# Layer norms spread into the stage before, a bound computed in pieces, buffers filled in pieces

## The chip, the cores and the metric

The kernel runs on one core of a Trainium2 chip. Its engines run in parallel, each with its own queue that is worked off in order: TensorE (PE: matmuls and transposes, with the load of its stationary operand shown apart as PEld), VectorE (DVE), ScalarE (ACT), GpSimd (POOL), and SyncE (SP), which here only starts DMA transfers. The metric is the device time of one execution in microseconds, the median of several.

## The reference, cut to what matters

Six layers are applied to x of 2 x 512 x 512 numbers in fp32, each behind a parameterless layer norm and with its input added back. In short:

```python
x = x + latent_attention_small(ln(x))   # 32 heads over latents of 12 and 4
x = x + ffn_lora(ln(x))                 # x @ W.T + bias, plus one adapter per batch
x = x + grouped_attention(ln(x))        # 32 heads of 128 in 8 groups, causal
x = x + ffn_lora(ln(x))
x = x + mla(ln(x))                      # 32 heads, low-rank q and kv, causal
x = x + ffn_moe(ln(x))                  # 8 adapters, the best 2 per row
x = x + attention_32x16(ln(x))          # 32 heads of 16, qkv bias, causal
x = x + ffn_moe(ln(x))
```

with

```python
def _layernorm(x, axis=-1, eps=1e-05):
    m = jnp.mean(x, axis=axis, keepdims=True)
    v = jnp.var(x, axis=axis, keepdims=True)
    return (x - m) / jnp.sqrt(v + eps)
```

The last attention masks with -66504 instead of minus infinity. Whether the masked entries can matter depends on the size of the weights: the kernel computes a bound from the norms of the q and k weights and takes one of two branches.

## The kernel before

x stays in on-chip memory as eight tiles of 128 rows by 512 (tiles 0 to 3 are the first batch, `b=0`; 4 to 7 the second). A **layer norm** of one tile (`layernorm`, L156 to L174) takes statistics on VectorE (L161, L163), an inverse square root (L179 on VectorE, L181 on POOL), xn = (x-m)*r on VectorE (L166, into one of two buffers), four 128x128 transposes on TensorE (L169), and a ScalarE copy into the shared room xT (L174). Every stage began with `layernorm_all`, all eight tiles in turn, and the LoRA, MoE and last-attention stages with `add_bias`, which adds the stage's output bias to x on POOL (L191). Chains of four accumulating matmuls go through `chain` (L150); their sum is added to x by VectorE in `add_to_x` (L194).

**Stages.** `attn_latent_small` works in 16 units (batch, half, i) under `run_quartets`, which interleaves scores of the next unit with exponents of this one; `divide`, `flatten` and `project` follow a unit as pieces. `ffn_lora` computes a coefficient from the start indices by seven small VectorE operations (L598 to L614), multiplies the adapter out (L619), adds it to the weight (L623) and runs one chain per tile. `attn_gqa` runs 16 (group, batch) steps m of four units j; `beside(m, j)` places values, outputs and keys between the units. `attn_mla` runs steps of eight heads h in the same manner. `ffn_moe` has a `front(t)` (router chain, the best two of eight on VectorE: L1051 to L1084) and a `back(t)` (transpose L1095, a chain of five), front one tile ahead of back. `causal_exact` (L1113) stands between MLA and the first MoE: it squares the two weights on POOL (L1131, 128x2048 each), sums over rows by two chains of four matmuls with a column of ones (`g_ones`), and leaves a flag. `attn_mha` first fills its rooms on POOL (qs, ks, vs, nm: L1179 to L1192), then per batch prepares q, k, v and runs `core`.

**What sets the order.** Inside `manual_schedule` blocks (the loops of the four attentions) TensorE's instructions stand in the order in which they are written; in MLA VectorE's also. Everything else is put in order by a planner that works with estimated durations and may move an instruction ahead of those written before it, but each engine still works its queue off in order. PSUM has eight banks, handed out by name (`proj`, `tr`, `sc`, `av`) or, inside the two big attentions, in turn (`hold`, `turn`, `release`). Large weights share five slots of 1 MB (tag w8), small ones six (w3); all loads are issued on SP's queue.

Of the kernel before, what the change touches and what calls it, by code (L numbers as in the profile page):

```python
# [38 lines left out]
P = 128  # L39
# [6 lines left out]
class Block:  # L46


    def __init__(self, ctx, tc, x, out):
# [10 lines left out]
        self.held = None  # L60

        self.x = []
        for t in range(NTILES):
            xt = self.const.tile([P, D], F32, tag=f"x{t}", name=f"x{t}")
            nc.sync.dma_start(out=xt, in_=x[t])
            self.x.append(xt)
# [10 lines left out]
        nc.gpsimd.memset(self.mhalf, -0.5)  # L77

# [77 lines left out]
    def layernorm(self, t, bank=None, back=False):  # L156

# [8 lines left out]
        nc.vector.tensor_scalar(xn, self.x[t], mv[:, 0:1], rstd, ALU.subtract, ALU.mult)  # L166
        tp = (bank or self.tr)()
# [7 lines left out]

    def inv_sqrt(self, v, scale, eps):

        ve = self.sm(1, "ve")
        self.nc.vector.tensor_scalar(ve, v, scale, eps, ALU.mult, ALU.add)  # L179
        r = self.sm(1, "rstd")  # L180
        self.nc.gpsimd.tensor_tensor(r, ve, self.mhalf, ALU.pow)  # L181
        return r

    def layernorm_all(self, bank=None, back=False):
        for t in range(NTILES):
            self.layernorm(t, bank, back)

    def add_bias(self, bias):

        for t in range(NTILES):  # L190
            self.nc.gpsimd.tensor_tensor(self.x[t], self.x[t], bias, ALU.add)  # L191
# [161 lines left out]
def attn_latent_small(k, a):  # L353
# [8 lines left out]
    with ExitStack() as ctx:  # L362
# [3 lines left out]
        wkvd = k.load(a["a_wkvd"], [P, KC, P], "w3", 6)  # L366
        wqk = k.load(a["a_wqk"], [P, 2, P], "a_wqk", 1, pool=lp)
# [84 lines left out]
        def fold_bias():  # L452
# [7 lines left out]
            k.add_bias(bias)  # L460

        folded = one([P, D], "folded")
        for piece in prepare(0):
            piece()
        extra = prepare(1) + [fold, fold_bias]
# [110 lines left out]

        with tc.manual_schedule(engines={mybir.EngineType.PE}):
            k.run_quartets(
                len(quartets), score, maxima, transposed, values, [divide, flatten, project], extra
            )  # L580


def ffn_lora(k, a):

# [3 lines left out]
    with ExitStack() as ctx:  # L588
# [6 lines left out]
        starts = k.load_row(a["f0_starts"], 4, "f0_starts", dtype=I32)  # L595
        rows = k.load(a["c_lora"], [P, 4], "c_lora", 1)

        startf = lp.tile([P, 4], F32, tag="startf", name="startf")  # L598
        nc.vector.tensor_copy(startf, starts)


        c = lp.tile([P, 4], F32, tag="le", name="le")
        nc.vector.tensor_scalar(c, startf, rows[:, 3:4], None, ALU.is_le)
# [938 lines left out]
```

## Time and profile before

| | |
|---|---|
| median of 3 runs | 2185.17 us (2184.05 to 2186.51) |
| profiled execution, its own time | 2187.9 us, span 2186.2 us, mean granted TensorE clock 0.98 |
| TensorE busy | 2083.8 us, 95% |
| VectorE, ScalarE, POOL busy | 1298.2, 731.3, 708.8 us |
| stages (start in us) | latent 0, LoRA 297, grouped 343, LoRA 1198, MLA 1244, bound and MoE 1738, last attention 1796, MoE 2125 |

A row of the view by stage has, behind the stretch, the busy time of each engine with the number of its instructions, then the granted clock as a share of full speed. A row of the timeline has start, duration, engine, line, operation, output and inputs, count, and in brackets how long the engine had been idle and what ended the idle time. A matmul in fp32 of 128 by 512 appears as two records. The whole in 40 slices, busy share in tenths:

```profile
PE   7999989999999999999998989999999889999988
PEld 3444444555555555555554444454544444554545
DVE  6678842655555555555555556666666584755745
ACT  2555621322222222222222155444544111541531
POOL 1100020423322222232322256555555436115211
```

### The profile page before, as it was taken

How to read it: one execution, taken by the hardware profiler on the slowest of the kernel's cores; microseconds unless marked ns; L12 is line 12 of the kernel's file. 1: busy time of each engine (PE TensorE's matmuls, PEld its weight loads, DVE VectorE, ACT ScalarE, POOL GpSimd, SP SyncE). 2: the span in 40 equal slices, each digit the busy share in tenths (PEclk: the TensorE clock that was granted, in tenths of full speed). 3: DMA queues.
4: the chain of work that ended last, by engine and by line, in shares of the span. 5: the costliest groups of instructions: out<-in, count | busy, mean ns of one | idle time of the engine just before them, and what ended most of it. 6: DMA issues, size and time to landing. Idle time of an engine off the chain costs nothing. (4 is left out here: it accounts for less than half of the span.)

```text
span 2186.2 us, 38883 instructions
## 1 busy us (share of the span) xinstructions
PE 2083.8 (95%) x15128; PEld 1094.9 (50%) x15128; DVE 1298.2 (59%) x3478; ACT 731.3 (33%) x2040; POOL 708.8 (32%) x945
## 2 busy tenths in 40 slices
PE   7999989999999999999998989999999889999988
PEld 3444444555555555555554444454544444554545
DVE  6678842655555555555555556666666584755745
ACT  2555621322222222222222155444544111541531
POOL 1100020423322222232322256555555436115211
PEclk9999989999999999999999999999999999999999
DMA  3000021112121212111010322010101102002001
GB/s 96 15 1 1 20 92 58 49 40 68 25 64 25 64 33 65 37 61 49 21 30 6 119 59 71 2 63 10 58 11 50 39 30 43 1 2 39 1 2 39
DMA packets 65751, 85.35 MB, mean 39 GB/s; under 512 B 13458, under 2 KB 50450, under 8 KB 60948
## 3 DMA queue, kind: packets, MB, share of 16 engines
q1 hardware_dynamic: 64916, 81.70, 12.6%
q8 instruction: 123, 2.02, 0.4%
q10 hardware_dynamic: 640, 1.05, 0.3%
q14 instruction: 72, 0.59, 0.1%
HBM read 58.60 MB, written 2.10 MB: 28 GB/s over the span
## 5 line engine op out<-in xcount | busy, mean ns | idle before, releaser
L239 ACT ACTIVATE room<-room,nmax 128x128 f32<-128x128 f32 (+3 forms) x384 | 211.2, 551 | 505.5 <-DVE nmax L229 504.5
L250 POOL TENSOR_SCALAR room<-room,invs 128x128 f32<-128x128 f32 (+3 forms) x384 | 198.0, 536 | 99.2 <-DVE invs L247 99.2
L677 POOL TENSOR_TENSOR q<-q,t 128x512 f32<-128x512 f32 x64 | 81.9, 1280 | 436.3 <-DVE t L676 436.3
L290 PE MATMUL sc<-turned,vals 32*128 32x128 f32 (+7 forms) x1058 | 190.6, 417 | 0.0
L290 PE MATMUL pj<-turned,vals 32*128 32x256 f32 (+7 forms) x692 | 189.0, 424 | 0.0
L290 PE MATMUL tp<-turned,vals 32*128 32x384 f32 (+7 forms) x676 | 158.8, 430 | 0.0
L218 PE MATMUL sc<-kT,q 128*32 128x256 f32 (+15 forms) x1576 | 145.6, 404 | 11.5 <-DVE invs L247 10.8
L263 DVE STREAM_TRANSPOSE turned<-room 128x1152 f32<-128x1152 f32 x80 | 107.9, 1363 | 73.1 <-POOL room L250 22.2
L290 PEld LDWEIGHTS sc<-turned,vals 32*128 32x128 f32 (+1 forms) x1058 | 126.3, 168 | 8.3 <-issue 5.6
L150 PE MATMUL pj<-room,w 128*128 128x512 f32 x272 | 122.2, 599 | 0.0
L181 POOL TENSOR_TENSOR rstd<-ve,mhalf 128x1 f32<-128x1 f32 x80 | 44.8, 562 | 205.3 <-DVE ve L179 192.4
L290 PEld LDWEIGHTS pj<-turned,vals 32*128 32x128 f32 (+1 forms) x692 | 107.1, 169 | 3.9 <-issue 2.2
L150 PE MATMUL sc<-w,room 128*128 128x512 f32 (+1 forms) x240 | 105.5, 582 | 0.0
L150 PE MATMUL sc<-room,w 128*128 128x512 f32 x232 | 105.2, 596 | 0.0
L290 PE MATMUL av<-turned,vals 32*128 32x256 f32 (+7 forms) x358 | 95.7, 420 | 8.8 <-DVE turned L263 8.8
L150 PE MATMUL sc<-w,ctxT 128*128 128x512 f32 x216 | 100.3, 607 | 2.2 <-ACT ctxT L304 2.2
L218 PE MATMUL tp<-kT,q 128*32 128x288 f32 (+15 forms) x1024 | 93.2, 398 | 2.9 <-POOL q L945 2.0
L290 PEld LDWEIGHTS tp<-turned,vals 32*128 32x128 f32 (+1 forms) x676 | 92.2, 169 | 4.4 <-issue 2.7
L239 ACT ACTIVATE probs<-probs,nmax 128x128 f32<-128x128 f32 (+3 forms) x128 | 71.1, 556 | 67.3 <-DVE nmax L229 66.0
L218 PEld LDWEIGHTS sc<-kT,q 128*32 128x32 f32 x1576 | 63.7, 110 | 58.4 <-issue 17.6
L218 PE MATMUL pj<-kT,q 128*32 128x256 f32 (+4 forms) x992 | 87.4, 386 | 4.9 <-DVE invs L247 4.1
L505 PE MATMUL sc<-qm,keys 32*128 32x512 f32 x200 | 86.8, 637 | 0.8 <-DVE qm L492 0.8
(564 smaller groups left out, 5768.8 us busy)
## 6 DMA issues: line engine op xcount, KB each, us to landing
vals<-v SPq DMA_DIRECT2D x256, 64.0 KB, 2.0
w<-in_b_wq SPq DMA_DIRECT2D x8, 1024.0 KB, 5.3
w<-in_b_wo SPq DMA_DIRECT2D x8, 1024.0 KB, 4.8
w<-in_m_wo SPq DMA_DIRECT2D x8, 1024.0 KB, 6.7
w<-in_f_w SPq DMA_DIRECT2D x4, 1024.0 KB, 4.8
w<-in_m_wqn SPq DMA_DIRECT2D x8, 384.0 KB, 3.1
x<-in_x SPq DMA_DIRECT2D x8, 256.0 KB, 4.6
w<-in_b_wk SPq DMA_DIRECT2D x8, 256.0 KB, 2.8
```

Source lines behind the costliest of these rows:

```text
L150: last = self.nc.tensor.matmul(out, lhsT, rhs, start=(i == 0), stop=(i == len(pairs) - 1))
L181: self.nc.gpsimd.tensor_tensor(r, ve, self.mhalf, ALU.pow)
L218: nc.tensor.matmul(ps[32 * i : 32 * i + 32, a - lo : b - lo], q[:, at : at + 32], keys[:, a:b], start=True, stop=True,)
L239: nc.scalar.activation(row, row, AF.Exp, bias=nmax, scale=-1.0, accum_out=total[:, qt : qt + 1])
L250: self.nc.gpsimd.tensor_scalar(row, row, inv[:, qt : qt + 1], 1.0, ALU.mult, ALU.mult)
L263: self.nc.vector.transpose(out[:, :last], probs[:, :last])
L290: self.nc.tensor.matmul(out[:, :, :n], values(i, j), rhs, start=(j == blocks[0]), stop=(j == stop[i]),)
L505: nc.tensor.matmul(ps, keys[b][rows[g], bass.ts(kc, P)], qm[u][rows[g]], start=True, stop=True)
L677: nc.gpsimd.tensor_tensor(out, out, t2, ALU.add)
```

## The change

The norm is split into `centred` (statistics and xn, optionally followed by the tile's bias add) and `place` (transposes and copy), and `layernorm_all` is gone. Tiles 0 to 3 of the next stage's norm are written into the end of the stage before: in the latent attention at units 7 to 9 of 16 (as the first batch is then complete), in the LoRA beside the chains of the second batch, in the grouped attention and MLA at the last step, in the MoE beside the second batch's tiles, in the last attention before the second `core`. Tiles 4 to 7 follow inside the stage itself. Bias adds go tile by tile. Only four tiles of x are loaded first; the other four behind two weights. The masks are built after the first `prepare`.

The LoRA coefficient is kept for the second use. PSUM banks are held in turn from the first LoRA to the end of MLA.

The bound becomes a class: its weights are loaded in the middle of the grouped attention, squared and summed over the four blocks on POOL in place, a piece per step, and one matmul with ones for each weight does the sum over rows. The flag is read before the last attention. The last attention's rooms are taken before the first MoE, which fills an eighth of each per tile on POOL.

```diff
-        self.x = []
-        for t in range(NTILES):
-            xt = self.const.tile([P, D], F32, tag=f"x{t}", name=f"x{t}")
-            nc.sync.dma_start(out=xt, in_=x[t])
-            self.x.append(xt)
+        self.coef = None
+        self.x = [
+            self.const.tile([P, D], F32, tag=f"x{t}", name=f"x{t}") for t in range(NTILES)
+        ]
+        self.source = x
+        self.load_x(0)
...
+        self.ones = self.const.tile([P, 1], F32, tag="ones", name="ones")
+        nc.gpsimd.memset(self.ones, 1.0)
+    def load_x(self, b):
+        for t in range(b * NT, b * NT + NT):
+            self.nc.sync.dma_start(out=self.x[t], in_=self.source[t])
+    def masks(self):
+        nc = self.nc
...
-    def layernorm(self, t, bank=None, back=False):
+    def centred(self, t, bias=None):
...
+        if bias is not None:
+            self.add_bias(t, bias)
+        return xn
+    def place(self, t, xn, bank=None, back=False):
+        nc = self.nc
...
+    def layernorm(self, t, bank=None, back=False, bias=None):
+        self.place(t, self.centred(t, bias), bank, back)
...
-    def layernorm_all(self, bank=None, back=False):
...
-    def add_bias(self, bias):
-        for t in range(NTILES):
-            self.nc.gpsimd.tensor_tensor(self.x[t], self.x[t], bias, ALU.add)
+    def add_bias(self, t, bias):
+        self.nc.gpsimd.tensor_tensor(self.x[t], self.x[t], bias, ALU.add)
...
+        k.load_x(1)
...
         for piece in prepare(0):
             piece()
+        k.masks()
...
+        normal = {}
+        def norms(u):
+            i = u - len(quartets) // 2 + 1
+            if i in (1, 2):
+                for t in (2 * i - 2, 2 * i - 1):
+                    k.place(t, normal.pop(t), k.turn)
+            if i in (0, 1):
+                for t in (2 * i, 2 * i + 1):
+                    normal[t] = k.centred(t)
+        after = [divide, flatten, project, norms]
         with tc.manual_schedule(engines={mybir.EngineType.PE}):
-            k.run_quartets(
-                len(quartets), score, maxima, transposed, values, [divide, flatten, project], extra
-            )
+            k.run_quartets(len(quartets), score, maxima, transposed, values, after, extra)
...
-        starts = k.load_row(a["f0_starts"], 4, "f0_starts", dtype=I32)
-        rows = k.load(a["c_lora"], [P, 4], "c_lora", 1)
-        startf = lp.tile([P, 4], F32, tag="startf", name="startf")
-        nc.vector.tensor_copy(startf, starts)
-        c = lp.tile([P, 4], F32, tag="le", name="le")
-        nc.vector.tensor_scalar(c, startf, rows[:, 3:4], None, ALU.is_le)
-        r = lp.tile([P, 3], F32, tag="rank", name="rank")
-        both = lp.tile([P, 2], F32, tag="both", name="both")
-        nc.vector.tensor_tensor(both, c[:, 1:3], c[:, 2:4], ALU.mult)
-        nc.vector.tensor_tensor(r[:, 0:2], c[:, 1:3], both, ALU.subtract)
-        nc.vector.tensor_copy(r[:, 2:3], both[:, 1:2])
-        nc.vector.tensor_tensor(r, r, rows[:, 0:3], ALU.mult)
-        coef = lp.tile([P, 1], F32, tag="coef", name="coef")
-        nc.vector.tensor_reduce(coef, r, AX.X, ALU.add)
-        nc.vector.tensor_scalar(la, la, coef, None, ALU.mult)
+        if k.coef is None:
...
+            nc.vector.tensor_reduce(k.coef, r, AX.X, ALU.add)
+        nc.vector.tensor_scalar(la, la, k.coef, None, ALU.mult)
...
-            out = [k.sc() for b in range(B)]
+            out = [k.turn() for b in range(B)]
...
-        k.layernorm_all()
-        k.add_bias(bias)
+        for t in range(NT):
+            k.add_bias(t, bias)
         for b in range(B):
             for t in range(NT):
-                ps = k.proj()
+                ps = k.turn()
                 k.chain(
                     ps, [(k.xT[b][:, c, bass.ts(t, P)], adapted[b][:, c]) for c in range(KC)]
                 )
                 k.add_to_x(b * NT + t, ps)
-def attn_gqa(k, a):
+                if b == 0:
+                    k.layernorm(NT + t, k.turn, bias=bias)
+                else:
+                    k.layernorm(t, k.turn, back=True)
...
-        k.hold()
-        k.layernorm_all(k.turn, back=True)
         ckvT = []
         for b in range(B):
+            if b:
+                for t in range(NT, NTILES):
+                    k.layernorm(t, k.turn, back=True)
...
+            if m == len(groups) and j in (1, 2):
+                for t in (2 * j - 2, 2 * j - 1):
+                    k.layernorm(t, k.turn)
...
+            for at, n in ((4, "q"), (9, "k")):
+                if (m, j) == (at, 2):
+                    bound.begin(n)
+                if m == at + 1:
+                    bound.square(j)
+                if (m, j) == (at + 2, 0):
+                    bound.sum()
+            if (m, j) == (12, 0):
+                bound.end()
...
-            k.hold()
-            k.layernorm_all(k.turn, back=True)
             for t in range(NTILES):
                 b, tt = divmod(t, NT)
+                if b == 0:
+                    k.layernorm(NT + t, k.turn, back=True)
...
+            last = m == len(groups)
+            if last and h == 0:
+                rows.extend(k.centred(t) for t in range(2))
+            if last and h == 1:
+                for t in range(2):
+                    k.place(t, rows[t], k.turn)
+                rows.extend(k.centred(t) for t in range(2, NT))
+            if last and h == 4:
+                for t in range(2, NT):
+                    k.place(t, rows[t], k.turn)
...
-        k.layernorm_all()
-        k.add_bias(bias)
+        for t in range(NT):
+            k.add_bias(t, bias)
...
-        prev = None
-        for t in range(NTILES):
-            hw = front(t)
-            if prev is not None:
-                back(*prev)
-            prev = (t, hw)
-        back(*prev)
...
-def ffn_moe(k, a, last=False):
+def ffn_moe(k, a, last=False, beside=lambda t: None):
...
+        rows = {}
+        for t in range(NTILES + 1):
+            if t < NTILES:
+                rows[t] = front(t)
+                beside(t)
+            if t < NT:
+                k.layernorm(NT + t, bias=bias)
+            if t > 0:
+                back(t - 1, rows.pop(t - 1))
+            if t > NT and not last:
+                k.layernorm(t - 1 - NT)
+class CausalBound:
...
+    def begin(self, n):
+        k = self.k
+        self.w = k.load(self.a["h_w" + n], [P, KC, D], "w8", 5)
+        self.row = k.w.tile([P, D], F32, tag="bias", name="bound", bufs=1)
+        k.nc.sync.dma_start(out=self.row[:1], in_=self.a["h_r" + n])
+    def square(self, c):
+        mul = lambda t: self.k.nc.gpsimd.tensor_tensor(t, t, t, ALU.mult)
+        mul(self.w[:, c])
+        if c:
+            self.k.nc.gpsimd.tensor_tensor(self.w[:, 0], self.w[:, 0], self.w[:, c], ALU.add)
+        else:
+            mul(self.row[:1])
+            self.k.nc.gpsimd.tensor_tensor(
+                self.w[:1, 0], self.w[:1, 0], self.row[:1], ALU.add
             )
+    def sum(self):
+        k = self.k
+        ps = k.turn()
+        k.chain(ps[:1], [(k.ones, self.w[:, 0])])
+        norm = k.sm(H, f"bound{len(self.norms)}", 1)[:1]
+        k.nc.vector.tensor_reduce(
+            norm, ps[:1].rearrange("p (h d) -> p h d", h=H), AX.X, ALU.add
+        )
+        self.norms.append(norm)
+    def end(self):
+        k, nc = self.k, self.k.nc
+        norm = self.norms[0]
+        nc.vector.tensor_tensor(norm, norm, self.norms[1], ALU.mult)
+        nc.vector.tensor_scalar(norm, norm, self.LIMIT, None, ALU.is_lt)
+        every = k.sm(1, "ve")[:1]
+        nc.vector.tensor_reduce(every, norm, AX.X, ALU.min)
+        self.flag = k.const.tile([1, 1], I32, tag="bound_flag", name="bound_flag")
+        nc.vector.tensor_copy(self.flag, every)
+    def register(self):
+        return self.k.nc.values_load(self.flag[0:1, 0:1], min_val=0, max_val=1)
+class HeadRooms:
...
+    def fill(self, i):
+        pool = self.k.nc.gpsimd
+        pool.memset(self.q[:, i], 0.0)
+        pool.tensor_copy(self.kk[:, i], self.column.broadcast_to([P, S]))
+        n = self.v.shape[1] // 8
+        pool.memset(self.v[:, i * n : (i + 1) * n], 1.0)
+        pool.memset(self.nm[i // 4][:, i % 4], 0.0)
...
+        for t in range(NT):
+            k.add_bias(t, bo)
...
             rotated(b, wq, bq, q, (nc.sync, nc.sync))
+            if b == 0:
+                for t in range(NT, NTILES):
+                    k.layernorm(t, bias=bo)
             last = rotated(b, wk, bk, kk, (nc.sync, nc.scalar))
...
             prepare(b)
+            if b:
+                for t in range(NT):
+                    k.layernorm(t)
...
     attn_latent_small(k, a)
+    bound = CausalBound(k, a)
+    k.hold()
     ffn_lora(k, a)
-    attn_gqa(k, a)
+    attn_gqa(k, a, bound)
     ffn_lora(k, a)
     attn_mla(k, a)
-    exact = causal_exact(k, a)
-    ffn_moe(k, a)
-    attn_mha(k, a, exact)
+    with k.tc.tile_pool(name="heads", bufs=1) as pool:
+        rooms = HeadRooms(k, a, pool)
+        ffn_moe(k, a, beside=rooms.fill)
+        attn_mha(k, a, bound.register(), rooms)
     ffn_moe(k, a, last=True)
```

## The prediction

> **What bounds the kernel.** I read the busy shares first (TensorE 2083.8 of 2186.2 us, 95%: at most 102.4 us of idle time can be won, plus what a lowered clock and removed work cost), then the busy time by stage, then the list of what TensorE waited for, then the timeline at each stage boundary. The stages, with columns start:end, length, then busy time of PE, PEld, DVE, ACT, POOL, the granted clock, DMA share and GB/s:
>
> ```profile
> 0.00:297.30 297.30, 276.62 (x1760) 123.80 (x1761) 207.80 (x366) 150.75 (x284) 24.93 (x39) 0.98 0.08 25
> ...
> 378.90:1198.30 819.40, 815.35 (x5924) 452.17 (x5921) 439.20 (x1030) 192.99 (x656) 240.58 (x345) 1.00 0.15 42
> 1198.30:1243.90 45.60, 42.13 (x113) 20.54 (x112) 27.09 (x56) 4.59 (x8) 12.42 (x14) 0.89 0.38 125
> ...
> 1738.50:1796.00 57.50, 52.75 (x196) 27.57 (x195) 45.84 (x176) 8.21 (x23) 14.82 (x16) 1.00 0.03 7
> 1796.00:1843.50 47.50, 40.20 (x109) 19.74 (x107) 24.09 (x35) 9.98 (x16) 42.25 (x28) 0.89 0.26 54
> ```
>
> The grouped attention (second row) has TensorE busy 99.5% of the time: nothing to win inside. The short stages are the ones with gaps and a clock below 1. The waits say who ends the gaps (total us, times, longest):
>
> ```profile
> PE tp L169 <- DVE xn L166: 17.2, 7, 6.7
> PE pj L169 <- DVE xn L166: 12.0, 3, 11.3
> ...
> PE av L290 <- DVE turned L263: 8.8, 2, 6.9
> ```
>
> 29.2 us stand ahead of the norm's transposes (L169): at a stage's head nothing but norms is ready. The 6.9 has another cause, on the timeline where the latent attention (MLA) ends (start, duration, what, idle before):
>
> ```profile
> 1704.58 3.60 POOL L1131 TENSOR_TENSOR room<-w 128x2048 f32<-128x2048 f32 x1 [2.23 <-DVE invs L247]
> ...
> 1708.16 2.06 POOL L250 TENSOR_SCALAR probs<-probs,invs 128x128 f32<-128x128 f32 x4
> ...
> 1711.68 1.11 PE L290 MATMUL av<-turned,vals 32*64 32x512 f32 x1 [6.89 <-DVE turned L263]
> ```
>
> A 3.60 us square for the bound (L1131) came ahead of the last softmax scaling on POOL's queue.
>
> **The change, boundary by boundary** (one norm: TensorE 0.44 us for four transposes; VectorE 0.69+0.18+0.14+0.54 = 1.55, with 0.55 on POOL between; a four-matmul chain of 512 columns 3.43).
>
> *Start.* TensorE first runs at 11.27 (the 11.3 above): VectorE takes statistics of several tiles (L161, up to 10.08) before its first xn at 10.68. Four tiles loaded first: about 3 us earlier, of which the deferred norms (4 x 1.55 on VectorE) give back 2 in the loop. **-1.**
>
> *Latent loop, norms of the next stage.* Added: 4 x 0.44 = 1.75 on TensorE and 4 x 1.55 = 6.2 on VectorE over three units. Between 131 and 300 us VectorE is busy 124 of 169 us and TensorE 162: a unit of about 14 us has 3.7 us of VectorE to spare, 11 over three, so the sum fits, but the transposes stand in a hand-written TensorE order and can wait. Ends: 1.75 (fits) and 10 (two groups each waiting some 4). By the row nearest (a maximum awaited for 1.9 us once), **+4.**
>
> *Into the first LoRA.* Idles 0.53 and 1.0 and 1.1 on L169 and cold clock (stage mean 0.85, about 4 us) for norms that will be done; the coefficient chain stays the first time. **-3.** *Into the grouped attention:* one idle of 0.75; **-0.5.**
>
> *Grouped attention into the second LoRA.* Between 1171 and 1216 about 14.9 us are lost: waits 1.87 and 2.17, half-clock stretches 1.7 and 1.8, 2.8 for norms behind the coefficient's small operations (L603, L606, L609), some 4.6 cold around L619 (8 matmuls 3.75, then 4.50). Kept coefficient and early norms remove the 2.8 and most of the last; the 1.87 stays; four norms fill most of the 2.17. I leave 8.2: **-6.7.** Here a rule is weighed. The clock rows:
>
> ```profile
> 1182.78 5.40 PE L150 MATMUL sc<-w,ctxT 128*128 128x512 f32 x8 [2.17 <-ACT ctxT L304]
> 1188.02 3.60 PE L150 MATMUL pj<-w,ctxT 128*128 128x512 f32 x8
> ```
>
> The Trainium skill ("TensorE: Matmul & The Clock Gate", Part 1) says that the clock halves after an idle window of about 3.4 us; by it a 2.17 us gap need cost nothing beyond itself, and this boundary would give -4.9. The row shows 1.8 us lost after a gap of 2.17; I follow the row.
>
> *The bound inside the grouped attention.* Two one-matmul sums replace two chains (7.03 us in 16 records at 1737.14): 7.03/4 = **+1.7** of TensorE there, and 18 POOL operations of 1.28 (the row of L677, same shape) = 23 us. Hidden: POOL is busy 241 of 819 us and the squares come one per step. A scaling delayed by 2 x 1.28 would show as a TensorE wait; taken as 0. Its two weights take one of the five w8 slots and shift their ring by one: the next group's wo then waits for the output of the group two back, which ends a step before, and lands 4.8 us later (row of in_b_wo), a step ahead of need, at a DMA share of 0.15: nothing. Likewise at nothing: the masks built later on POOL (their first reader is 300 us away), the second half of x behind two weights on SP's queue (0.25 MB a tile, 4.6 us, needed a unit later), the register read moved past the first MoE (its flag is then 500 us old).
>
> *Second LoRA into MLA.* Eight norms stand ahead of the first chain's end at 1251; afterwards the four of the second half lie between chains paced 3.4 us by the small operations. **-3.**
>
> *MLA, bound, first MoE, head of the last attention* (1703.7 to 1811). The square leaves POOL: 6.89 becomes about 3.3, **-3.6**, the scaling and turn themselves being late next. The bound's chains: **-7.0**, with their small VectorE work behind which norms waited (0.77 and 1.78, the latter on g_flag): **-2.** Norms of the last attention go into the MoE loop; at 1796 they cost:
>
> ```profile
> 1795.86 3.52 POOL L1179 MEMSET qs<- 128x4096 f32 x1 [1.91 <-PE sc L150]
> ...
> 1796.44 6.94 DVE L166 TENSOR_SCALAR xn<-x,ln_mv,rstd 128x512 f32<-128x512 f32 x2
> 1799.31 3.79 POOL L1181 COPY ks<-c_spare 128x4096 f32<-128x4096 f32 x1
> 1799.80 0.63 PE L169 MATMUL tp<-ident,xn 128*128 128x128 f32 x4 [3.13 <-DVE xn L166]
> ...
> 1803.53 1.09 PE L169 MATMUL tp<-ident,xn 128*128 128x128 f32 x4 [3.10 <-DVE xn L166]
> ```
>
> Idles 3.13+3.10+1.07, about 4 of cold clock, 1.75 of transposes: the gap to close is **-13**. But the MoE loop pays. Where it already carries a norm per tile it runs at 6.36 us a tile (hw transposes at 1764.42 and 1770.78), against 5.33 of TensorE (front 0.93, back 4.40). Before, some tiles carry none; after, all eight do: about **+6** with the first router chain of some 5 us now uncovered. The fills add 3.52+3.79+2.22+1.54 = 11.07 us of POOL, 1.38 a tile. The second rule is weighed here, the one that speaks against the change: the skill ("SBUF — State Buffer", Who interferes with whom) says that POOL and a two-port VectorE operation lock each other out for a whole instruction. By it every fill could be paid, 8 x 1.38 = 11. The rows agree on the mechanism (xn 3.47 each here, 0.51 elsewhere), but in the loop just one operation per tile shows it: hotp takes 1.00 beside a 1.27 bias add, 0.23 without. 8 x 0.5 = **+4.** Sum -15.5, ends -7 and -23.
>
> *Last attention and second MoE.* Four norms beside the second prepare: +1.75 of TensorE, where it is full (41.30 of 41.30). After the last attention TensorE stood 6.66 us for a norm (2132.51) and then ran cold; about 5 of it stays, for the first router chain is now what is late; norms of tiles 4 to 7 lie in the loop. **-3.**
>
> **Sum:** -1+4-3-0.5-6.7+1.7-3-15.5-3 = -27.0. From the profiled execution's 2187.9 (span 2186.2 and 1.7 around it): 2160.9; that run lies 2.7 above the median of the runs shown (2185.17), so the median goes to **2158**; the forecast's own range is 2147 to 2170. No change means within 0.2%, 4.4 us, which is about what a measurement of this kernel can tell.
>
> **Rivals.**
> 1. *Mostly given back* (chance 0.18): the latent loop costs 10, fills 10, the LoRA heads keep part of their cold clock (4 less won): -27+6+6+4 = -11, **2174**. For it: VectorE's 45.84 of 57.5 in MoE. Against: VectorE's spare time in the latent loop.
> 2. *Everything hidden* (0.15): fills free (-4), latent loop 1.75 (-2), both MoE at TensorE's 5.33 a tile (12 tiles with norms x 1.0, -12), boundary before the second LoRA clean (-5): -27-23 = -50, **2135**. Against: the 6.36 a tile that exists already.
> 3. *Slower* (0.08): norms put into the hand-written TensorE order stand in it until xn is there, and everything behind stands too. Seven such groups (two in the latent loop, two where grouped attention ends, two where MLA ends, one before the second core). At the 6.66 seen at 2132.51 each: 7 x 6.66 = 46.6, net +20, **2205**. It decides from (27+4.4)/7 = 4.5 us each. Against: statistics start as soon as x is complete, a step ahead of the transposes.
> 4. *It does not do what it says* (0.05): the order outside the hand-written parts is planned, and statistics are hoisted already (L161 at 1171.16, before the last values); two xn buffers then hold the norms where they were. Only the bound's 7 and the kept coefficient's 2 remain, less its sums' 1.7, 1.75 before the second core and 4 of fills: -1.5, **2184**, no change.
>
> **Chances.** Forecast 0.54. Faster: 0.54+0.18+0.15 = 0.87; same 0.05; slower 0.08. Range 2136 to 2177: it takes in most of rival 1 and the near half of rival 2, leaving out rivals 3 and 4 and the rest.
>
> **What would show it.** Right: first transposes near 8; none of the three L169 waits above 3 us left but the last MoE's; no chain with g_ones, and the last MLA wait about 3.3; MoE tiles near 6.4 to 6.9; the last attention's head at clock 1. Wrong: waits on xn inside the latent or grouped loops; MoE tiles above 8 us; softmax scaling late beside the bound's squares.

## The result, and the profile after

| | before | changed |
|---|---|---|
| median, beside each other | 2185.84 us (2184.05 to 2188.02, 4 runs) | 2155.49 us (2154.52 to 2156.56, 4 runs) |
| profiled execution: its own time, span | 2187.9, 2186.2 | 2156.43, 2154.7 |
| mean granted TensorE clock | 0.980 | 0.987 |
| TensorE busy | 2083.8 | 2068.3 |

The ratio is 0.9861, 95% interval 0.9844 to 0.9878: 30 us faster. The forecast was 2158. A second comparison of the same two kernels gave 0.9834 (0.9818 to 0.9851). A difference of some 0.003, 6 us, between medians therefore says little here; for the small steps I go by the trace, and compare times from one landmark to the next, not absolute ones. Where an edit leaves a short stretch alone, such a time comes back: from MLA's last query to the last attention's first score, the nine traces in which that stretch is unedited lie between 143.4 and 143.5 us. The long loops vary more, by up to 5 us.

Busy time by stage, changed kernel (columns as in the view shown of before; the stretches are grouped attention, second LoRA, first MoE, second MoE):

```profile
378.50:1197.70 819.20, 816.20 (x5943) 451.80 (x5940) 443.57 (x1041) 194.99 (x660) 264.13 (x366) 1.00 0.16 46
1197.70:1232.00 34.30, 34.30 (x109) 16.42 (x109) 20.56 (x45) 4.11 (x7) 5.73 (x8) 1.00 0.48 167
...
1720.60:1772.60 52.00, 46.32 (x181) 26.19 (x180) 42.35 (x167) 7.83 (x23) 25.09 (x47) 1.00 0.03 6
...
2092.90:2150.60 57.70, 49.52 (x161) 27.32 (x160) 33.91 (x151) 5.67 (x20) 7.17 (x8) 0.88 0.09 33
```

The second LoRA went from 45.60 us at clock 0.89 to 34.30 us at clock 1.00, with TensorE busy throughout. The last stage still runs at 0.88. TensorE's waits (total us, times, longest), changed kernel:

```profile
PE pj L186 <- DVE xn L175: 11.6, 1, 11.6
...
PE tp L186 <- DVE xn L175: 4.8, 2, 4.3
PE sc L650 <- DVE w L643: 4.7, 1, 4.7
```

Of 29.2 us of waits for xn, 16.7 are left (0.3 of it in a row not shown), nearly all at the very start (11.6) and at the head of the second MoE (4.3). The third row is new: the adapter's products of the first LoRA (L650) wait for VectorE's scaling of A (L643).

Where the 31.4 us between the two spans came from, from landmark to landmark of the two traces:

| stretch | before | changed | measured | forecast |
|---|---|---|---|---|
| start to the first latent score | 26.47 | 28.97 | +2.5 | -1 |
| latent attention | 270.84 | 273.03 | +2.2 | +4 |
| first LoRA | 45.80 | 41.26 | -4.5 | -3 |
| head of the grouped attention | 35.87 | 35.28 | -0.6 | -0.5 |
| grouped attention, bound's sums in it | 819.34 | 819.12 | -0.2 | +1.7 |
| second LoRA | 45.58 | 34.34 | -11.2 | -6.7 |
| head of MLA, to its third query | 46.76 | 47.88 | +1.1 | -3 |
| MLA to its last output | 446.24 | 440.67 | -5.6 | -3.6 |
| bound's chains and first MoE | 58.70 | 52.05 | -6.6 | -9 +6 +4 = +1 |
| head of the last attention, to its first score | 55.70 | 44.23 | -11.5 | -13 |
| last attention, second MoE | 334.8 | 337.9 | +3.1 | -3 |

The sum was off by some 4 us, but its terms by up to 7.6, in both directions: they err by 15 us on the one side and by 19 on the other, and that these nearly cancel is luck.

### The profile page after: what moved, and what is told of

It reads as the page before. It is cut to its first block, busy times and chain, and to the rows that moved or that the text cites. A ratio compares the mean times of both kernels' runs of the same rounds, so it can differ in the third digit from the quotient of the medians.

```text
span 2154.7 us, 38870 instructions
## 1 busy us (share of the span) xinstructions
PE 2068.3 (96%) x15116; PEld 1085.4 (50%) x15116; DVE 1281.2 (59%) x3467; ACT 728.8 (34%) x2040; POOL 719.2 (33%) x988
## 5 line engine op out<-in xcount | busy, mean ns | idle before, releaser
L305 PE MATMUL sc<-turned,vals 32*128 32x256 f32 (+7 forms) x1004 | 187.3, 420 | 0.0
L305 PE MATMUL tp<-turned,vals 32*128 32x384 f32 (+7 forms) x742 | 170.9, 411 | 0.0
L305 PE MATMUL pj<-turned,vals 32*128 32x384 f32 (+7 forms) x754 | 146.8, 416 | 3.1 <-DVE turned L278 3.1
L233 PE MATMUL sc<-kT,q 128*32 128x160 f32 (+15 forms) x1536 | 139.5, 399 | 8.6 <-DVE invs L262 7.9
L278 DVE STREAM_TRANSPOSE turned<-room 128x1152 f32<-128x1152 f32 x80 | 108.0, 1363 | 66.4 <-POOL room L265 22.1
L305 PEld LDWEIGHTS sc<-turned,vals 32*128 32x128 f32 (+1 forms) x1004 | 122.5, 167 | 6.2 <-issue 4.1
L305 PEld LDWEIGHTS tp<-turned,vals 32*128 32x128 f32 (+1 forms) x742 | 102.9, 167 | 5.0 <-issue 2.7
L305 PEld LDWEIGHTS pj<-turned,vals 32*128 32x128 f32 (+1 forms) x754 | 97.8, 169 | 11.8 <-DVE turned L278 5.8
L233 PE MATMUL tp<-kT,q 128*32 128x224 f32 (+15 forms) x1032 | 92.4, 392 | 6.9 <-DVE invs L262 6.9
L233 PE MATMUL pj<-kT,q 128*32 128x512 f32 (+4 forms) x992 | 92.7, 407 | 2.9 <-POOL q L993 1.9
L160 PE MATMUL sc<-w,ctxT 128*128 128x512 f32 x192 | 87.5, 598 | 0.0
L265 POOL TENSOR_SCALAR probs<-probs,invs 128x128 f32<-128x128 f32 (+3 forms) x128 | 65.6, 532 | 61.3 <-DVE invs L262 57.4
```

The lines of the kernel that those rows point to most:

```text
L160: last = self.nc.tensor.matmul(out, lhsT, rhs, start=(i == 0), stop=(i == len(pairs) - 1))
L233: nc.tensor.matmul(ps[32 * i : 32 * i + 32, a - lo : b - lo], q[:, at : at + 32], keys[:, a:b], start=True, stop=True,)
L265: self.nc.gpsimd.tensor_scalar(row, row, inv[:, qt : qt + 1], 1.0, ALU.mult, ALU.mult)
L278: self.nc.vector.transpose(out[:, :last], probs[:, :last])
L305: self.nc.tensor.matmul(out[:, :, :n], values(i, j), rhs, start=(j == blocks[0]), stop=(j == stop[i]),)
```

## The experiments

All edits are to the changed kernel. The ratio is to the kernel before, run beside each.

| run | edit | median us | ratio (95%) |
|---|---|---|---|
| c0 | none | 2153.29 | 0.9834 (0.9818 to 0.9851) |
| e1 | bound whole again, behind MLA | 2168.05 | 0.9901 (0.9885 to 0.9918) |
| e2 | fills whole again | 2161.74 | 0.9869 (0.9852 to 0.9885) |
| e3 | MLA's norms ahead of its chains | 2150.40 | 0.9824 (0.9807 to 0.9840) |
| e4 | three banks for the adapter | 2160.67 | 0.9866 (0.9850 to 0.9882) |
| e5 | last MoE's norms back at its head | 2153.95 | 0.9843 (0.9826 to 0.9859) |
| e6 | second LoRA's norms back at its head | 2155.24 | 0.9845 (0.9828 to 0.9861) |
| e7 | second batch's norms held at the start | 2153.81 | 0.9848 (0.9830 to 0.9867) |
| e8 | last attention's norms back at its head | 2158.51 | 0.9854 (0.9838 to 0.9871) |
| e9 | coefficient computed twice | 2159.32 | 0.9864 (0.9848 to 0.9881) |
| e11 | three edits together | 2147.20 | 0.9805 (0.9789 to 0.9822) |
| e12 | the three, placed better | 2143.30 | 0.9797 (0.9783 to 0.9811) |

**e1, the bound.** The pieces in the grouped attention are dropped, and `causal_exact` of before stands again ahead of the first MoE:

```diff
-                if m == at + 1:
-                    bound.square(j)
...
+    exact = causal_exact(k, a)
     ffn_moe(k, a, beside=rooms.fill)
```

> The changed kernel (2155.5), but the bound computed where it was, between MLA and the first MoE, in two chains of four with POOL squares of 128x2048. Theory: the move was worth 7.0 us of chains and about 3.6 us of the scaling that stood behind the square, less 1.7 us of sums in the grouped attention: 8.9 slower, about 2164; a MLA wait on the turned probabilities near 6.9 us comes back. Rival (the chains lay beside waits for norms that are gone, so little is lost): at most 4 slower, below 2160.

The first transposed router result (hw) of the MoE came 13.9 us after its place in the changed kernel, the span grew by 10.7, and this ratio's interval alone of the undoing runs lies above both of the changed kernel's. POOL's and TensorE's timeline where MLA ends, in e1:

```profile
1691.88 3.60 POOL L1243 TENSOR_TENSOR room<-w 128x2048 f32<-128x2048 f32 x1 [2.86 <-DVE invs L262]
1695.46 2.05 POOL L265 TENSOR_SCALAR probs<-probs,invs 128x128 f32<-128x128 f32 x4
...
1698.98 1.11 PE L305 MATMUL av<-turned,vals 32*64 32x512 f32 x1 [4.79 <-DVE turned L278]
```

and in the changed kernel:

```profile
1692.82 2.05 POOL L265 TENSOR_SCALAR probs<-probs,invs 128x128 f32<-128x128 f32 x4 [2.96 <-DVE invs L262]
...
1696.34 0.64 PE L305 MATMUL pj<-turned,vals 32*64 32x512 f32 x1 [1.28 <-DVE turned L278]
```

In e1 POOL was free at 1691.88 and took the square first; the last scaling stood behind it. TensorE's wait for that value (L305 on `turned`, L278) is 4.8 in e1 and 1.3 in the changed kernel. Behind the wait a record of the same shape takes 1.11 us instead of 0.64: the granted clock is 0.50 from there to 1703.9 in e1, and 1.00 throughout this place in the changed kernel. By stretches, e1 is 7.4 us longer from MLA's last query to its last output, 7.3 longer from there to the first hw, and 2.0 shorter from the first hw to the last. Of the 7.4, 3.5 are the longer wait, 1.4 a new wait for an xn, and some 2.4 the clock (an estimate: half of the 4.9 us at half clock). So 12.8 us are lost up to the last attention's first score. The theory holds in kind, and was too small: it had 8.9, with a wait near 6.9 and no loss of clock.

**e2, the fills.** `beside=rooms.fill` goes, and the rooms are filled whole at the head of the last attention, as before; only their allocation stays ahead of the MoE:

```diff
+        nc.gpsimd.memset(q, 0.0)
+        nc.gpsimd.tensor_copy(
+            kk.rearrange("p t s -> p (t s)"), rooms.column.broadcast_to([P, 8 * S])
+        )
...
-        ffn_moe(k, a, beside=rooms.fill)
+        ffn_moe(k, a)
```

> The changed kernel, but the rooms of the last attention filled whole at its head, not an eighth per MoE tile. Theory (my step: fills cost 4 in the MoE loop, and at the head 11 us of POOL stand ahead of the bias adds and the rotation): MoE shorter by about 4, head longer by 4 to 8, 0 to 4 slower, about 2157. Rival (each fill locks VectorE out for its whole length, 8 x 1.38): the MoE loop gets 11 shorter and the kernel about 5 faster, 2150.

The edit did not put the fills back where they had been: the planner moved them by itself to the MoE's beginning, since their rooms were free there. In e2's timeline (start, duration):

```profile
1730.82 3.60 POOL L1275 COPY ks<-c_spare 128x4096 f32<-128x4096 f32 x1
1730.87 3.56 DVE L1132 SCALAR_TENSOR_TENSOR rest<-hotp,p 128x8 f32<-128x8 f32 x1
```

and in the changed kernel's:

```profile
1729.00 0.79 POOL L1255 COPY ks<-c_spare 128x512 f32<-128x512 f32 x1
...
1729.25 0.56 DVE L1118 TENSOR_SCALAR hotp<-cand,first 128x8 f32<-128x8 f32 x1
```

A VectorE operation on eight columns, 0.15 to 0.23 us elsewhere, ends with POOL's copy in both: it waits as long as that copy lasts. Behind a piece the wait is at most 0.8. In e2 TensorE waited 5.66 us for the first router result, in the changed kernel 2.58. From MLA's last query to the first score e2 took 146.5 us against 143.4: compared with whole fills in the MoE, the pieces are worth some 3 us. What whole fills at the attention's head would cost beside early norms, as both theories had it, no run shows. Another 3.7 of e2's longer span (2163.3) came between MLA's first and last query, where its trace shows a granted clock of 0.76 against 0.95 over the first 34 us, and which the edit does not touch. Its median alone tells nothing.

**e8, norms of the last attention.** The norms written beside the first MoE's second batch go back to the next head, fills stay in pieces:

```diff
-            if t > NT and not last:
-                k.layernorm(t - 1 - NT)
...
-            k.add_bias(t, bo)
+            k.layernorm(t, bias=bo)
```

> The changed kernel, but the last attention's norms of tiles 0 to 3 written at its own head, not into the first MoE's second half; fills stay in pieces. Theory (what made the old head slow was the whole fills on POOL, xn 3.47 beside them and 0.51 otherwise, not where the norms stood): 0 to 3 slower than the changed kernel (ratio 0.985 to 0.986). Rival (the norms' place is worth the 11.5 that this head gained): 7 or more slower, ratio 0.988 or more.

From MLA's last output to the first score it took 98.4 us against 96.3: 2.1. That is a balance: from the last hw to the first score, the head alone, e8 is 3.9 us longer, and the MoE before it 1.7 shorter from its first hw to its last. With the fills gone TensorE waits for these norms 1.5 us at the head, in two pieces, where it had waited 3.13+3.10+1.07 before (xn of 3.47 us each beside the big fills). So of the 11.5 us that this head gained some 4 are the norms' place; the rest I put down to the fills, by subtraction, since e2 did not bring them back there.

**e4, banks.** The adapter's products get three fixed banks, as many as before had under the name sc:

```diff
-            out = [k.turn() for b in range(B)]
+            out = [k.held[(0, 3, 6)[(2 * m + b) % 3]] for b in range(B)]
```

> The changed kernel, but both LoRAs put their adapter products into three of the held PSUM banks only, as before, not eight in turn. Theory: the eight banks let the products of the two batches run at the same time (second LoRA, 16 records: 3.6 us after, 8.9 with gaps before), so each LoRA loses about 4: 2163. Rival (VectorE was late because of the norms that stood there, not for lack of banks): less than 1 slower, 2156.

TensorE where the second LoRA starts, in e4:

```profile
1202.41 1.98 PE L650 MATMUL sc<-w,w 48*128 48x512 f32 x6
1204.65 3.69 PE L650 MATMUL sc<-w,w 48*128 48x512 f32 x10 [0.26 <-DVE adapted L654]
```

and in the changed kernel, where each bank has its own row:

```profile
1197.73 0.69 PE L650 MATMUL tp<-w,w 48*128 48x512 f32 x1
1197.74 0.69 PE L650 MATMUL sc<-w,w 48*128 48x512 f32 x1
...
1201.37 3.70 PE L160 MATMUL tp<-adapted,room 128*128 128x512 f32 x8
```

The products of the two batches start 0.01 us apart and run together; eight pairs of records take 3.64 us. With three banks a product waits for VectorE's add that empties one, and the same 16 records take 5.86, at a clock of 1. The first LoRA, in e4:

```profile
306.31 8.94 PE L650 MATMUL sc<-w,w 48*128 48x512 f32 x16 [0.92 <-DVE w L643]
```

In the changed kernel these 16 records took 5.84 us. Here the clock has a part as well (0.52 granted in e4, 0.63 in the changed kernel over the products), and the first chain behind them is longer too: the stage is 5.2 us longer than in the changed kernel, 0.7 longer than before the change. Over both LoRA stages, from the first product of the one to the last of the other, e4 is 7.4 us longer. Its median lies within the spread, so the gain is shown in the trace only.

**e9, the coefficient; e6, the norms ahead of the second LoRA.**

```diff
-        if k.coef is None:
+        if True:
```

> The changed kernel, but the LoRA coefficient computed again in the second LoRA by the seven small VectorE operations. Theory (their chain starts only when the grouped attention's room is free, and the products wait for it as in the first LoRA, 4.65): 3 to 5 slower, ratio 0.986 to 0.987, with a wait of 2 to 4.7 us ahead of the second LoRA's products. Rival (it is worked off ahead, beside the last output chains): no wait, under 1 slower.

```profile
1201.41 0.67 PE L650 MATMUL tp<-w,w 48*128 48x512 f32 x1 [3.16 <-DVE w L643]
...
1203.86 1.06 PE L650 MATMUL pj<-w,w 48*128 48x512 f32 x1
```

The first product waits 3.16 us for L643, and after two pairs at 0.59 to 0.69 us a record five pairs run at 0.74 to 1.06 (granted clock 0.58, then 0.50): the last product is 4.9 us later than in the changed kernel (898.9 against 894.0 us from the first LoRA's first product). The theory holds.

```diff
+        if k.coef is not None:
+            for t in range(NT):
+                k.layernorm(t, k.turn)
...
-            if m == len(groups) and j in (1, 2):
-                for t in (2 * j - 2, 2 * j - 1):
-                    k.layernorm(t, k.turn)
```

> The changed kernel, but the second LoRA's norms of tiles 0 to 3 at its own head, not in the last step of the grouped attention. Theory (the boundary gained 11.5 where I had 5, and taking the banks away gave 6.9 of it back in the trace, so some 4 to 5 are the norms): 4 to 6 slower. Rival (the norms alone are what made the boundary slow: VectorE's xn stood between the adapter sums): 8 or more slower.

Nothing: 893.6 us against 894.0 over the same stretch, so theory and rival both failed. Written back in the head, the norms' transposes still ran at 1179.92 and 1195.14, between the last output chains: the planner put them there itself.

**e3, MLA's head.** All four norms of the second half ahead of the first chain:

```diff
+            for t in range(NT, NTILES):
+                k.layernorm(t, k.turn, back=True)
             for t in range(NTILES):
-                if b == 0:
-                    k.layernorm(NT + t, k.turn, back=True)
```

> The changed kernel, but MLA's norms of tiles 4 to 7 all ahead of its first chain, not one beside each chain. Theory from the two traces (this head took 1.2 us more after the change): about 1 faster, 2154 to 2155. Rival (my prediction: tiles beside chains save 3): 3 slower, 2158.5.

The third query comes 2.8 us earlier from the end of the second LoRA. Changed kernel (transposes of successive tiles' y, L913, and the norm between, L186):

```profile
1240.26 0.33 PE L186 MATMUL sc<-ident,xn 128*128 128x128 f32 x1 [0.27 <-DVE xn L175]
...
1241.57 0.33 PE L913 MATMUL tp<-ident,y 128*128 128x128 f32 x1
...
1245.68 0.33 PE L913 MATMUL tp<-ident,y 128*128 128x128 f32 x1 [0.54 <-DVE y L894]
```

A tile takes 4.11 us with a norm in it. In e3 the starts are 1239.25, 1242.62, 1246.05, 1249.35: 3.4 a tile. A chain of small operations on VectorE, with POOL and ScalarE between, sets the pace there (TensorE waits for its y at most tiles); VectorE itself is idle for some 2 of the 4.11 us. A norm lengthens the chain by 0.7: xn (0.54 us) and the start of the inverse root (0.14) stand between two of its links. The statistics had been taken earlier.

**e5, the last MoE's norms** back from before the second `core` to the head of the last MoE:

```diff
+        if last:
+            for t in range(NT):
+                k.layernorm(t)
...
-            if b:
-                for t in range(NT):
-                    k.layernorm(t)
```

> The changed kernel, but the last MoE's norms of tiles 0 to 3 at that MoE's head, not before the last attention's second core. Theory from the traces (the last MoE took 57.7 us after and 57.3 before, because VectorE works norms of tiles 4 and 5 before the router of tile 0, whoever did tiles 0 to 3): 1.75 us come back before the core and 2 to 4 are lost at the head: 0 to 2 slower than the changed kernel. Rival (my prediction: the move saves 4.75 at the head): 3 slower.

No difference in the median; in the trace the last attention from first score to last is 3.6 us shorter, the rest 1.0 longer. (The first of these stretches took 245.2 to 248.3 us in traces where it is unedited, 243.3 here, so the 3.6 is not certain.) TensorE stands 6.68 us for a norm again and 3.06 for the first router result; with the norms early it stands 4.31 and 3.87. The rival, 3 slower, did not come. What is late, in the changed kernel and in order of time:

```profile
2094.88 0.69 DVE L170 BATCH_NORM_STATS2 ln_stats<-x 128x6 f32<-128x512 f32 x1 [2.14 <-issue]
...
2097.25 1.11 PE L186 MATMUL tp<-ident,xn 128*128 128x128 f32 x4 [4.31 <-DVE xn L175]
...
2101.57 0.16 DVE L1127 TENSOR_REDUCE nmax<-pj 128x1 f32<-128x8 f32 x1
```

VectorE norms tiles 4 and 5 and takes the statistics of 6 and 7 before it begins the routing of tile 0 (L1127), whose logits had long been there.

**e7, the start.** Norms of tiles 4 to 7 are held until xn of tile 3:

```diff
+                with tc.issue_after(first):
+                    k.layernorm(NT + t, k.turn)
```

> The changed kernel, but the statistics of tiles 4 to 7 held back on VectorE until the xn of tile 3 is issued. Theory: the start gained nothing because the planner put those statistics, which wait for x tiles landing up to 8.8 us, ahead of the first xn (10.97 us, though its inverse root was there at 5.9); held back, the first xn comes near 8 and the first score 4 to 6 earlier: 2150 to 2152 on the first chip. Rival (the weights of the first chain or the tiles themselves land too late for more): less than 1.5 earlier.

The first transposes came at 8.22 us instead of 11.55, but not the 4 to 6 us at the first score. They came with gaps, tile 3 behind another load, and the first chain took 6.54 us, against 3.70 in c0: first score at 27.2 against 26.0 in c0 and 29.0 in the execution shown, whose first chain was slow too (6.21). In these two slow chains a weight load takes 0.34 us, in c0's 0.19, the durations of half and full clock; that the clock's column has 1.00 there says nothing, for the traces hold no record of the clock before 14.6 us (c0) or 19.6 and 21.1 (the other two). Slow chain against slow chain e7 is 1.8 us earlier, against c0 it is 1.2 later: what the edit is worth stays open. In the ten traces whose start is the changed kernel's the first score came between 26.0 and 29.6 us.

**c0** is the changed kernel once more:

> The changed kernel again, as the yardstick for the other runs beside it: a ratio of 0.986 to the kernel before, and within about 3 us the same stage times as in its first profile.

**e11 and e12, an order that mends what was found.** e11 joins e3's edit with the coefficient computed in the latent attention and each norm of both MoE stages held behind the routing of a tile four before:

```diff
+        def scale():
+            with tc.issue_after(k.late):
+                k.adapter = adapter(k, a)
-        extra = prepare(1) + [fold, fold_bias]
+        extra = prepare(1) + [fold, fold_bias, scale]
...
-                k.layernorm(NT + t, bias=bias)
+                with tc.issue_after(k.routed):
+                    k.layernorm(NT + t, bias=bias)
```

> Built on what the runs showed: the changed kernel with MLA's norms all ahead of its first chain, the LoRA coefficient and scaled A made inside the latent attention, and VectorE's norm of tile 4+t held behind the router of tile t in both MoEs. Theory: 3.3 at MLA's head, 4.65 and a cold stretch at the first LoRA, 2 to 4 in the MoEs, about 11 faster than the changed kernel, ratio 0.979 to 0.981. Rival (gaps closed at one place open at the next, or the clock takes them back): under 4 faster, ratio above 0.982.

From the end of the second LoRA to MLA's third query e11 is 2.7 us shorter and from the last score to the end 6.0, but from MLA's last output to the first score 2.8 longer, and the coefficient only moved: first LoRA -6.0, latent loop +5.6. In e11 the coefficient's operations fell beside POOL's bias adds:

```profile
97.16 1.27 POOL L207 TENSOR_TENSOR x<-x,bias_all 128x512 f32<-128x512 f32 x1 [82.37 <-DVE startf L626]
97.20 1.26 DVE L628 TENSOR_SCALAR le<-startf,c_lora 128x4 f32<-128x4 f32 x1
```

`adapter` is the coefficient's code with the scaling of A, and `late` the sum that makes the folded bias. e12 puts `scale` ahead of `fold` and sets `late` at the second batch's cq, so ahead of those adds; e12 holds the norms in the last MoE only:

> The changed kernel with three placements mended: all eight norms of MLA's input ahead of its first chain; the coefficient and the scaled A made in the latent attention, right behind the cq of its second batch and ahead of GpSimd's bias adds; in the last mixture of experts alone each tile's norm held behind the router of the tile four before it. Theory (the three losses are separate and none is only moved): MLA's third query 3.3 to 3.6 us earlier from the end of the second LoRA, as in the run with that edit alone; no wait of 4.65 us of the first LoRA's products for VectorE and no more than 1 us added in the latent loop, since GpSimd's bias adds no longer lie beside the small operations; last mixture of experts about 4.9 shorter, and the first one as in the changed kernel (no 2.8 us added). Together about 12 us below the changed kernel, ratio to the kernel before 0.978 to 0.981. Rival (closed gaps come back elsewhere: the latent loop pays for the coefficient wherever it stands, and the tiles of the last mixture wait for their norms at its end): ratio 0.982 or more, and the latent loop's end over 3 us later than in the changed kernel.

The same operation in e12:

```profile
71.39 0.22 DVE L628 TENSOR_SCALAR le<-startf,c_lora 128x4 f32<-128x4 f32 x1
```

From first score to last projection the latent loop takes 273.5 us (changed kernel 272.6), the first product follows 0.5 us later (5.2), the end of the second LoRA to MLA's third query is 2.7 shorter (3.3 to 3.6 were expected), MLA's first query to its last 404.6 (408.4), the first MoE's first hw to the first score 88.2 (88.2), last score to last hw 76.3 (82.4), with a granted clock of 1.00 from the last score to 2137 us (0.92 in the changed kernel over the same place). The span is 2138.9 against 2154.7. At 2143.3 us, ratio 0.9797 (0.9783 to 0.9811), e12 is faster than both kernels; its interval lies below both of the changed kernel's, while the size of the gain over it, 8 to 14 us from the ratios and 15.8 from the traces, is less certain. The rival's ratio did not come.

## Why the prediction was right, and where its steps were not

The time was right, 2.5 us off; of its steps some were right, and the errors of the others nearly cancelled. Two slips in its working change nothing: the group from MLA's end to the last attention's head adds to -15.6, not -15.5, and the idle of 0.75 us ahead of the grouped attention is two, of 0.36 and 0.39. Step by step:

- **Start, -1: wrong.** Statistics stayed ahead of xn: the planner put those of tiles 4 to 6, which wait for their loads until 8.77, before the first xn (10.97), whose own rstd was done at 5.9. The +2.5 itself says nothing about the change, since the start varies by more (e7).
- **Latent loop, +4:** 2.2, inside its ends.
- **First LoRA, -3:** -4.5, but as a balance the step did not contain. The norms' waits went (the third of them was 2.11 us in the trace of before, which the step reads as 1.1) and the products paired; the coefficient, until then worked off between the norms, was laid bare: 4.65 us of wait and a cold start. The step "the coefficient chain stays" priced it at nothing because the norms covered it. e4 shows that with three banks, and the longer half clock behind them, the stage gains nothing; e12 shows that without the bare coefficient it gains 6.0 more, 4.7 of it wait, and then runs at clock 1.00 instead of 0.92.
- **Second LoRA, -6.7: mis-sized, -11.2.** I read L619's 3.75+4.50 us in the trace of before as cold clock alone. The term that failed is the 8.2 left: at full clock three banks still need 5.86 where the new ones need 3.64 (e4). The coefficient was worth 4.9 (e9). These two make 7.1 of the 11.2; the rest no run took back. The early norms as written were worth nothing (e6): the planner hoists them itself, which I put down to the banks being held across the stages, untested. This hoisting was the fourth rival's mechanism, and it was true here.
- **Bound in the grouped attention, +1.7:** TensorE's busy time rose by some 0.9 and its idle time there fell by as much (4.0 to 3.0); net -0.2. The POOL squares cost nothing that shows.
- **MLA's head, -3: wrong sign.** The step laid norms "between chains paced 3.4 us by the small operations" as if these left room for a norm on VectorE. It was their chain that it lengthened: e3 shows 2.8 us lost.
- **MLA's end and the bound, -3.6-7.0-2 = -12.6: right as a sum,** 12.8 by e1, and luck in its parts. MLA's end was worth 7.4, not 3.6: the step left out the half clock behind the wait (some 2.4, an estimate from e1) and an xn that came late (1.4). The chains with their small work were worth 5.3 up to the last hw, not 9. The scaling itself was less late than thought, 1.3 instead of 3.3.
- **First MoE, +10: far too high.** The stretch gained 6.6, of which e1, which keeps these norms and fills, gives back 5.3; so by this balance the step's own norms and fills cost nothing that shows. I took one stretch of 6.36 us as the price of every tile with a norm; the trace after has 3.2, 7.7, 6.9, 5.4 and 5.8 from hw to hw. And I spread the fills over eight tiles; the planner ran all of them between 1720.8 and 1736.4 beside the first router chains, where TensorE waits for a result once for 2.58 us and once for 1.73.
- **Head of the last attention, -13: right in size (-11.5),** but some 4 of it are the norms' place (e8), and the rest, by subtraction, the fills'.
- **Last attention and second MoE, -3: wrong, +3** (335.0 to 339.1 us over the ten traces that leave these stages as they are, 334.8 before). "The first router chain is now what is late" was half of it: it is late since VectorE norms later tiles first. e5 shows that moving the norms won nothing; holding later norms back (e11, e12) gave 6.

The **two rules.** The clock: the row of before did show a loss after a gap of 2.17 us, against the 3.4 us of the Trainium skill ("TensorE: Matmul & The Clock Gate", Part 1), and in e9 a gap of 3.16 us was paid for too. But I took one row for a rule. The wait of 1.87 us at the end of the grouped attention's last step stands in all fourteen traces, and in four of them, that of before among them, a half-clock stretch follows; the changed kernel's gap of 2.58 us ahead of the first hw cost none (clock 1.00 in the view by stage), and the same gap in e7 did (0.50 from 1726.3 to 1729.7). Gaps of 3.36 (e11) and 3.25 (e12) in the last MoE cost none; all gaps above 3.8 us behind the start, in every trace, had one. So a gap of 2 to 3.4 us may or may not cost, and no run here tells beforehand which. The locking of VectorE by POOL (the Trainium skill, "SBUF — State Buffer", Who interferes with whom): the mechanism is in every row shown (3.56 beside 3.60, 1.26 beside 1.27, 0.56 within 0.79); that POOL's operations were short is worth some 3 us of its price (e2). Both prices that I weighed, 11 and 4, were too high by the balance of the first MoE; no run leaves the fills out.

Of the rivals, the first (mostly given back) was right in kind on the first LoRA's new wait and the late second MoE, the second (everything hidden) on the first MoE and the second LoRA at full clock; neither held everywhere. No hand-placed norm stalled TensorE anywhere near the 4.5 us from which the third decides; the planned, not hand-placed, last MoE did (4.3).

**Open.** How much of the first LoRA's gain is the banks themselves and how much the clock behind them, and what the latent loop's +2.2 consists of, no run tells apart. How far the start varies was seen in single executions only.

## What to carry to other kernels

Before moving work under cover, ask which engine is the cover's own pace: a norm beside a TensorE chain is free only if the chain isn't waiting for the engine that does the norm (e3, and the rows of the last MoE in e5). When a wait in front goes, look at what it was covering; the coefficient cost little until the norms had left. Where a planner orders the work, the freedom to move (a free bank, a room allocated early) can be worth more than the place at which work is written (e2, e4, e6), and work that waits for data may be put ahead of work that is ready.

## What the hardware showed unasked

- Two products on 48 partitions each, of different batches, run at the same time when each has a bank free: 16 records in 3.64 us; 5.86 with three banks in turn, where they wait for VectorE's adds.
- Whether POOL holds up a small VectorE operation depends on both. A SCALAR_TENSOR_TENSOR of eight columns that began beside a copy or an add of 128x512 or more lasted until that one ended in all 91 cases of the traces (3.56 us instead of 0.15 beside the copy of 128x4096 in e2); beside a MEMSET of 128x512 in none of 12. A TENSOR_SCALAR of four or eight columns was held by all three: in 44 of 44 cases beside copies and adds (1.26 us instead of 0.22 in e11), in 5 of 5 beside a MEMSET (2.11 in e2). A reduction of eight columns and a reciprocal kept their 0.16 and 0.15 us beside that same MEMSET in e2. Counted are operations that began with 0.3 us or more of POOL's still to come.
- At the program's start the same chain of eight records took 3.70 us in one execution of a kernel and 6.21 in another, behind transposes in one row; behind scattered ones 6.54.
- Every half-clock stretch that these traces record, apart from the last, which reaches past the program's end, lasts 3.41 us or a multiple of it. It can begin 1.1 us after a gap of 3.16 us has ended (e9: records of 0.59 us, then of 1.06) or 0.07 us after one of 2.17 (before, 1182.78).
